# Edge rows of a forward Fourier stage: loaded once, copied on the chip, multiplied last

## The chip, the cores and the metric

The kernel runs on one core of one Trainium2 chip. A core has a matrix engine (TensorE, PE in the profile, with its weight loads listed as PEld), a vector engine (VectorE, DVE), a scalar engine (ScalarE, ACT), a general engine (GpSimd, POOL) and a sync engine (SyncE, SP), each with its own queue of instructions that it takes in order. Sixteen DMA engines move data between HBM and the on-chip memory; a DMA is issued from the queue of one of the engines (here SP, POOL and, for constants, ACT).

The metric is the device time of one execution in microseconds, the median of several executions.

## What is computed

The reference has two layers on a tensor of 4 batches x 512 time steps x 128 x 64. The first layer (normalisations, a decayed scan, two convolutions, a small feed-forward net) isn't touched by the change. The second takes a moving average over time as a trend, mixes the lowest 128 Fourier modes of the remainder with complex weights, and adds both up:

```python
trend = _moving_average(x, KERNEL)      # 25 steps, ends repeated
seasonal = x - trend
xf = jnp.fft.rfft(seasonal, axis=1)
xs = xf[:, :M]                          # M = 128
ys = jnp.einsum('bmnc,cmk->bknc', xs, W)
...
filt = jnp.fft.irfft(yf, n=T, axis=1)
return trend + filt
```

## The kernel before

The second layer is `layer1`. It goes over the four batches in two groups of two (lines 959 to 965). For each group it runs `transform` for both batches, then `mix`, then `invert` for both. All of it is in float32. The products of one group stay in one large on-chip tile `xf`.

`transform` (line 834) is the forward Fourier transform. One batch is cut along its 8192 columns into NS = 16 slabs of SL = 512 columns, so a group has 32 slabs and the whole kernel 64. For a slab:

- `slab` (line 827) loads all 512 time steps of the columns, 1 MB, on SP's queue into a tile `xin`. The pool tag `big` has five buffers.
- A tile `edge` (line 839, pool tag `edge`, two buffers) receives the first 12 and the last 12 time steps of the columns, because the moving average treats the ends of the time axis differently from a circular one and these 24 rows carry the correction. Lines 840 to 842 load the 24 rows twice, to partitions 0 to 23 and to partitions 32 to 55: four DMAs of 24 KB each (12 rows of 2 KB), on POOL's queue. One copy of the rows meets the weights of the real part, the other those of the imaginary part (r = 0 and 1); partitions 32 to 55 are what the profile calls the second row group.
- VectorE folds the time axis: sums and differences `uv` of the halves (line 846, two instructions), then sums and differences `ev` of the quarters of the sum (line 856, two instructions). Each of the tags has two buffers.
- TensorE makes three sets of products into two PSUM tiles `pf[0]` and `pf[1]`. Called E, D and V here: E, the edge products (line 853), four matmuls with 24 rows, which open the sums (`start=True`); D, the odd modes from the differences (line 860), four matmuls onto one half of each `pf`; V, the even modes (line 867), four matmuls onto a quarter each. Every float32 matmul appears twice in the profile, so the profile has eight of each for a slab. The PSUM tag `a` has four buffers, which is two slabs.
- ScalarE copies `pf[0]` and `pf[1]` into `xf` (line 871).

TensorE takes its instructions in the order of the code (`manual_schedule`, line 958): E, D, V of one slab, then E, D, V of the next. The other engines' queues are ordered by the framework's scheduler, which may place an instruction ahead of one from an earlier line. A tile's buffer is written again only when all its readers are done: the loads of `edge` for slab s wait for E of slab s-2, `uv` of slab s for D of slab s-2, and the first product of slab s for the copies of slab s-2 to `xf`.

`mix` (line 873) loads 1 MB of weights at a time into `w`, which shares the tag `big` with `xin` and so waits for old slabs, and negates parts of it on POOL (line 882). `invert` (line 905) goes back to time: per slab it makes the waves, loads `xin` again, loads `halo` rows on SP into the tag `edge` (lines 937 and 940), forms the moving average (lines 943 and 946), adds (line 949) and writes 1 MB out on POOL's queue (line 950).

Of the kernel before, what the change touches and what calls it, by code (L numbers as in the profile page):

```python
# [17 lines left out]
T = 512  # L18
NF = 128
H = 64  # L20
# [10 lines left out]
HALO = KMA // 2  # L31
# [748 lines left out]
def layer1(ctx, tc, x4, wri, dftv, dftd, dfte, idfte, idfto, avg, avgh, out):  # L780
# [7 lines left out]
    nc = tc.nc  # L788
# [9 lines left out]
    def load(name, src):  # L798
        t = const.tile(list(src.shape), F32, name=name)
        nc.scalar.dma_start(t, src)  # L800
        return t

    dftv_sb = load("dftv_sb", dftv)
    dftd_sb = load("dftd_sb", dftd)
    dfte_sb = load("dfte_sb", dfte)
# [5 lines left out]
    def bank(tag):  # L811
        return ps.tile([P, SL], F32, tag=tag, name=tag)


    def by_c(row):
        return row.rearrange("p (a c l) -> p a l c", c=H, l=2)

    def by_n(row):
        return row.rearrange("p (a l c) -> p a l c", c=H, l=2)
# [7 lines left out]
    def slab(b, s):  # L827
        xin = io.tile([P, NT, SL], F32, tag="big", name="xin", bufs=5)
        nc.sync.dma_start(
            xin, x4[b][:, s * SL : (s + 1) * SL].rearrange("(c p) d -> p c d", p=P)  # L830
        )
        return xin

    def transform(b, xf):

        for s in range(NS):
            c = slice(s * SL, (s + 1) * SL)
            xin = slab(b, s)
            edge = io.tile([P, SL], F32, tag="edge", name="edge")
            for r in range(2):  # L840
                nc.gpsimd.dma_start(edge[32 * r : 32 * r + HALO, :], x4[b][0:HALO, c])
                nc.gpsimd.dma_start(edge[32 * r + HALO : 32 * r + 2 * HALO, :], x4[b][T - HALO : T, c])
            uv = []
            for op in (ALU.add, ALU.subtract):
                t = io.tile([P, 2, SL], F32, tag=f"uv{len(uv)}", name="uv")
                nc.vector.tensor_tensor(t, xin[:, 0:2, :], xin[:, 2:4, :], op)  # L846
                uv.append(t)
            pf = [bank("a"), bank("a")]
            for r in range(2):
                at = slice(32 * r, 32 * r + 2 * HALO)  # L850
                for h in range(2):
                    hs = slice(h * H, (h + 1) * H)
                    nc.tensor.matmul(pf[r][hs, :], lhsT=dfte_sb[at, hs], rhs=edge[at, :], start=True, stop=False)  # L853
            ev = io.tile([P, 2, SL], F32, tag="ev", name="ev")
            for k, op in enumerate((ALU.add, ALU.subtract)):
                nc.vector.tensor_tensor(ev[:, k, :], uv[0][:, 0, :], uv[0][:, 1, :], op)
            for i in range(2):
                for r in range(2):
                    h = 1 - r
                    nc.tensor.matmul(  # L860
                        pf[r][h * H : (h + 1) * H, :], lhsT=dftd_sb[:, i, r, :], rhs=uv[1][:, i, :],
                        start=False, stop=(i == 1),
                    )
            for k in range(2):
                for r in range(2):
                    q = r * H + k * H // 2
                    nc.tensor.matmul(  # L867
                        pf[r][q : q + H // 2, :], lhsT=dftv_sb[:, k, r, :], rhs=ev[:, k, :], start=False, stop=True
                    )
            for r in range(2):  # L870
                nc.scalar.copy(by_c(xf[:, r, c]), by_n(pf[r]))

# [85 lines left out]
    with tc.manual_schedule(engines={nc.tensor.engine}):  # L958
        for b0 in range(0, B, G):
            xf = spec.tile([P, G, 2, D], F32, tag="xf", name="xf")  # L960
            for b in range(G):
                transform(b0 + b, xf[:, b, :, :])
            mix(xf)
            for b in range(G):
                invert(b0 + b, xf[:, b, :, :])
# [109 lines left out]
```

## Time and profile before

| | us |
|---|---|
| median of 3 executions | 3868.74 (3863.71 to 3873.1) |
| the profiled execution, own time | 3868.33 |
| its span in the profile | 3866.3 |
| TensorE busy in it | 3643.1 (94%) |
| VectorE busy | 2695.6 (70%) |
| ScalarE busy | 1722.6 (45%) |
| GpSimd busy | 567.9 (15%) |
| all E products, both stages (81.0), D (129.6), V (70.9) | 281.5 |
| first transform stage, first product to the first product of `mix` | 2868.89 to 3004.77 |
| second transform stage, likewise | 3363.38 to 3503.36 |

The page has one row for each engine and a picture of the span in 40 slices. Below that it lists, for groups of equal instructions, the busy time, the mean duration of one, and the idle time just before them with what ended it. A group's busy time counts overlapping instructions once, while the mean is that of one instruction: the 512 edge products have a mean of 626 ns, and yet are busy for 81.0 us, because four of them run side by side on different parts of the array. Of the whole span, the two transform stages, which the change touches, are about 276 us.

### The profile page before, as it was taken

What the parts mean: (1) busy time and instruction counts of PE and PEld (TensorE: products, weight loads), DVE (VectorE), ACT (ScalarE), POOL (GpSimd) and SP (SyncE); (2) the same over time, 40 slices, a digit from 0 to 9 for tenths busy, and PEclk for the clock granted to TensorE, in tenths of its full rate; (3) what the DMA queues carried; (4) which work ended last, traced back from release to release, by engine and by line L of the source; (5) the groups of instructions that cost most, each with busy time, mean ns of one, the idle gap of its engine ahead of it and who ended that gap; (6) DMA issues with size and microseconds to landing.
All of it is one profiled execution on the core that took longest, in us unless ns stands there. A gap on an engine that the chain in (4) does not pass through costs nothing. (4 is left out here: it accounts for less than half of the span.)

```text
span 3866.3 us, 44881 instructions
## 1 busy us (share of the span) xinstructions
PE 3643.1 (94%) x15945; PEld 1343.5 (35%) x15945; DVE 2695.6 (70%) x3498; ACT 1722.6 (45%) x2427; POOL 567.9 (15%) x910
## 2 busy tenths in 40 slices
PE   9999999988999999899999988999989999999999
PEld 4433322233333223333322322333322843326533
DVE  4445669978656896865689799855558267792577
ACT  0023346645556564555656578867742210022100
POOL 0000012211000121110012121100025101141011
PEclk9999999999999999999999999999989999999999
DMA  9767657777765787776568677645559468994587
GB/s 310 262 215 251 222 181 260 258 242 273 255 229 183 235 279 259 248 257 231 191 229 274 215 252 248 213 162 179 182 192 289 145 217 293 314 295 157 191 299 266
DMA packets 432695, 913.86 MB, mean 236 GB/s; under 512 B 36248, under 2 KB 86616, under 8 KB 428376
## 3 DMA queue, kind: packets, MB, share of 16 engines
q1 hardware_dynamic: 350080, 634.55, 49.3%
q0 software_dynamic: 79872, 274.77, 20.3%
q8 instruction: 127, 2.08, 0.2%
q10 hardware_dynamic: 2520, 1.67, 0.1%
q14 instruction: 96, 0.79, 0.1%
HBM read 642.35 MB, written 268.50 MB: 236 GB/s over the span
## 5 line engine op out<-in xcount | busy, mean ns | idle before, releaser
L667 PE MATMUL pa<-mid,w_sb 128*64 128x512 f32 x2048 | 505.9, 615 | 74.0 <-DVE x4t L672 73.5
L660 ACT ACTIVATE mid<-m,fb_sb 128x1024 f32<-128x1024 f32 x256 | 284.5, 1111 | 245.0 <-PE m L656 244.5
L672 DVE SCALAR_TENSOR_TENSOR x4t<-pa,fb_sb,x 128x512 f32<-128x512 f32 x252 | 187.7, 745 | 200.5 <-PE pa L667 200.5
L656 PE MATMUL m<-x,w_sb 64*128 64x512 f32 x1008 | 291.7, 651 | 1.0 <-ACT mid L660 0.7
L660 ACT ACTIVATE mid<-c,fb_sb 128x1024 f32<-128x1024 f32 x256 | 283.0, 1106 | 1.2 <-PE c L656 1.1
L667 PEld LDWEIGHTS pa<-mid,w_sb 128*64 128x64 f32 x2048 | 126.3, 138 | 421.3 <-issue 223.8
L656 PE MATMUL c<-x,w_sb 64*128 64x512 f32 x1008 | 264.1, 597 | 4.7 <-ACT mid L660 4.7
L360 PE MATMUL a<-xp,wx 128*128 128x512 f32 x512 | 246.5, 608 | 6.2 <-DVE wx L357 5.7
L943 PE MATMUL b<-xin,avg_sb 128*128 128x512 f32 x512 | 230.8, 593 | 3.3 <-DVE xin L949 3.3
L949 DVE TENSOR_TENSOR xin<-b,pm 128x512 f32<-128x512 f32 x256 | 159.2, 683 | 96.4 <-PE b L946 81.5
L920 ACT COPY two<-a 128x512 f32<-128x512 f32 x64 | 37.5, 585 | 424.1 <-PE a L915 424.1
L523 ACT ACTIVATE sq<-x 128x1024 f32<-128x1024 f32 x128 | 134.9, 1054 | 200.6 <-DVE x L520 200.6
L564 DVE SCALAR_TENSOR_TENSOR to<-kd,vec,to 128x510 f32<-128x510 f32 (+1 forms) x288 | 210.7, 744 | 18.7 <-ACT to L560 16.9
L633 ACT ACTIVATE kd<-kd,vec 128x512 f32<-128x512 f32 x256 | 193.5, 809 | 7.1 <-DVE kd L625 7.1
L846 DVE TENSOR_TENSOR uv<-xin 128x1024 f32<-128x1024 f32 x128 | 156.3, 1226 | 46.9 <-PE a L860 30.1
L250 PE MATMUL st<-x,ones 128*32 128x512 f32 x512 | 173.7, 606 | 13.8 <-DVE x L520 13.5
L344 DVE BATCH_NORM_STATS2 stt<-wx 128x6 f32<-128x512 f32 x174 | 113.1, 685 | 101.2 <-DMA wx<-in_x 100.7
L825 DVE COPY xf<-b 128x256 f32<-128x256 f32 x128 | 54.4, 425 | 183.2 <-PE b L889 182.6
L681 PEld LDWEIGHTS pt<-ident,x4t 128*128 128x128 f32 x1024 | 108.3, 141 | 210.9 <-ACT mid L660 155.0
L692 POOL DMA_DIRECT2D x<-ob x64 | 49.0, 766 | 899.9 <-ACT ob L688 853.6
L357 DVE TENSOR_SCALAR wx<-wx,vec 128x192 f32<-128x192 f32 x174 | 48.8, 318 | 189.0 <-DMA wx<-in_wkvr 170.9
L482 PE MATMUL a<-rst,wo_sb 64*128 64x512 f32 x512 | 150.5, 662 | 30.8 <-DVE x L484 28.6
(238 smaller groups left out, 6803.4 us busy)
## 6 DMA issues: line engine op xcount, KB each, us to landing
xp<-in_xt SPq DMA_DIRECT2D x256, 512.0 KB
xin<-x SPq DMA_DIRECT2D x128, 1024.0 KB
kh<-to SPq DMA_DIRECT2D x152, 512.0 KB
x<-x POOLq DMA_DIRECT2D x128, 512.0 KB, 4.0
kx<-x SPq DMA_DIRECT2D x128, 512.0 KB
x<-ob POOLq DMA_DIRECT2D x64, 1024.0 KB, 6.6
out<-xin POOLq DMA_DIRECT2D x64, 1024.0 KB, 7.1
x<-x SPq DMA_DIRECT2D x96, 512.0 KB
```

Of the source, the lines that this page charges most:

```text
L250: nc.tensor.matmul(st[32 * q : 32 * q + 32, :], lhsT=ones, rhs=src[:, j, :], start=first, stop=last,)
L360: nc.tensor.matmul(pa[:, k, :], lhsT=wq[:, j, k * P : (k + 1) * P], rhs=xp[:, j, :], start=first and j == 0, stop=last and j == 1,)
L482: nc.tensor.matmul(at[:, j, :], lhsT=wo_sb[js, :], rhs=rst[js, :], start=True, stop=True)
L564: nc.vector.scalar_tensor_tensor(to[:, j, k:], xr[:, j, : SL - k], vec[:, w, c], to[:, j, k:], ALU.mult, ALU.add)
L633: tc.keep_in_program_order(nc.scalar.activation(d[:, j, :], d[:, j, :], AF.Identity, bias=vec[:, B4, c], scale=vec[:, G4, c]))
L656: nc.tensor.matmul(pm[:, h, :], lhsT=w1_sb[hs, m * P : (m + 1) * P], rhs=x3[hs, :], start=True, stop=True)
L660: nc.scalar.activation(mid, pm, AF.Gelu_apprx_tanh, bias=fb1_sb[:, m : m + 1])
L667: nc.tensor.matmul(pa[h * H : (h + 1) * H, :], lhsT=w2_sb[:, m, :], rhs=mid[:, h, :], start=(m == 0), stop=(m == 1),)
L672: nc.vector.scalar_tensor_tensor(x4t, pa, fb2_sb, x3s[c // 2][:, c % 2, :], ALU.add, ALU.add)
L846: nc.vector.tensor_tensor(t, xin[:, 0:2, :], xin[:, 2:4, :], op)
L943: nc.tensor.matmul(po[j], lhsT=avg_sb[:, j, :], rhs=xin[:, j, :], start=True, stop=False)
L949: nc.vector.tensor_tensor(by_n(xin[:, j, :]), by_n(po[j]), by_c(pm[j % 2][:, j // 2, :]), ALU.add)
```

## The change

The 24 edge rows are loaded once, to partitions 0 to 23, with two DMAs in place of four. ScalarE then copies them to partitions 32 to 55. The edge products move from the first place in a slab to the last: D and V now open the sums, and E closes them.

```diff
             edge = io.tile([P, SL], F32, tag="edge", name="edge")
-            for r in range(2):
-                nc.gpsimd.dma_start(edge[32 * r : 32 * r + HALO, :], x4[b][0:HALO, c])
-                nc.gpsimd.dma_start(edge[32 * r + HALO : 32 * r + 2 * HALO, :], x4[b][T - HALO : T, c])
+            nc.gpsimd.dma_start(edge[0:HALO, :], x4[b][0:HALO, c])
+            nc.gpsimd.dma_start(edge[HALO : 2 * HALO, :], x4[b][T - HALO : T, c])
+            nc.scalar.copy(edge[32 : 32 + 2 * HALO, :], edge[0 : 2 * HALO, :])
...
             pf = [bank("a"), bank("a")]
-            for r in range(2):
-                at = slice(32 * r, 32 * r + 2 * HALO)
-                for h in range(2):
-                    hs = slice(h * H, (h + 1) * H)
-                    nc.tensor.matmul(pf[r][hs, :], lhsT=dfte_sb[at, hs], rhs=edge[at, :], start=True, stop=False)
...
                     nc.tensor.matmul(
                         pf[r][h * H : (h + 1) * H, :], lhsT=dftd_sb[:, i, r, :], rhs=uv[1][:, i, :],
-                        start=False, stop=(i == 1),
+                        start=(i == 0), stop=False,
                     )
...
                     nc.tensor.matmul(
-                        pf[r][q : q + H // 2, :], lhsT=dftv_sb[:, k, r, :], rhs=ev[:, k, :], start=False, stop=True
+                        pf[r][q : q + H // 2, :], lhsT=dftv_sb[:, k, r, :], rhs=ev[:, k, :], start=True, stop=False
                     )
+            for r in range(2):
+                at = slice(32 * r, 32 * r + 2 * HALO)
+                for h in range(2):
+                    hs = slice(h * H, (h + 1) * H)
+                    nc.tensor.matmul(pf[r][hs, :], lhsT=dfte_sb[at, hs], rhs=edge[at, :], start=False, stop=True)
```

The built program shows where the scheduler puts things. ScalarE's queue now has the copy for slab s+1 ahead of the two `xf` copies of slab s (copy 0, copy 1, `xf` 0, copy 2, `xf` 1, and so on). POOL's queue has two loads for a slab in place of four; the first negation of `w` stood ahead of the loads of the last three slabs of a group, and now stands ahead of those of the last four. SP's queue is the same, and VectorE's too, but for one `uv` instruction per group that moves by one place. TensorE's queue is the same list with one E (four matmuls) taken from the front of each group's transform and put at its end.

## The prediction

> **What bounds the kernel now.** I read first the groups of instructions for TensorE, then the order of time in a calm part of the first transform stage, then the edge loads one at a time, then the two ends of the second stage.
>
> The groups of instructions, shapes kept apart (form, count, busy us, mean ns, idle before):
>
> ```profile
> L860 PE MATMUL a<-uv,dftd_sb 128*64 128x512 f32 x512 | 129.6, 628 | 0.0
> L853 PE MATMUL a<-edge,dfte_sb 24*64 24x512 f32 x512 | 81.0, 626 | 21.8 <-DMA edge<-x 21.8
> L867 PE MATMUL a<-ev,dftv_sb 128*32 128x512 f32 x512 | 70.9, 627 | 0.0
> L846 DVE TENSOR_TENSOR uv<-xin 128x1024 f32<-128x1024 f32 x128 | 156.3, 1226 | 46.9 <-PE a L860 30.1 <-DMA edge<-x 14.3 <-DMA xin<-x 0.6
> L871 ACT COPY xf<-a 128x512 f32<-128x512 f32 x128 | 73.5, 630 | 234.1 <-PE a L867 234.1
> ```
>
> Only E ever waits for data that TensorE can't hurry (21.8 us; the first 16 are the stage's cold start). One calm slab in order of time (start, busy, instruction, idle before):
>
> ```profile
> 2961.90 1.09 PE L853 MATMUL a<-edge,dfte_sb 24*64 24x512 f32 x8
> 2962.05 1.15 ACT L871 COPY xf<-a 128x512 f32<-128x512 f32 x2 [2.73 <-PE a L867]
> 2962.92 1.94 PE L860 MATMUL a<-uv,dftd_sb 128*64 128x512 f32 x8
> 2963.31 0.50 POOL L841 DMA_DIRECT2D edge<-x  x1 [1.89 <-PE a L853]
> 2964.78 1.07 PE L867 MATMUL a<-ev,dftv_sb 128*32 128x512 f32 x8
> 2964.80 0.51 POOL L842 DMA_DIRECT2D edge<-x  x1
> 2965.78 1.09 PE L853 MATMUL a<-edge,dfte_sb 24*64 24x512 f32 x8
> ```
>
> E takes 1.02 us, D 1.86, V 1.00: a period of 3.88 us without a gap, so TensorE is the bound here. VectorE is close behind (two `uv` of 1.226 and two `ev` of 0.69: 3.83 by the means), and a window over two such slabs has the DMA engines at a share of 0.94. Everything is nearly level, and the edge loads are too: issued 0.32 us after E of slab s ends, the last of the four 1.49 later, they have until E of slab s+2. Where this fails, E is longer or late:
>
> ```profile
> 2892.85 1.40 PE L853 MATMUL a<-edge,dfte_sb 24*64 24x512 f32 x8
> ...
> 2897.04 1.39 PE L853 MATMUL a<-edge,dfte_sb 24*64 24x512 f32 x8
> ...
> 3363.38 1.97 PE L853 MATMUL a<-edge,dfte_sb 24*64 24x512 f32 x4
> ...
> 3367.40 1.97 PE L853 MATMUL a<-edge,dfte_sb 24*64 24x512 f32 x4 [2.05 <-DMA edge<-x]
> 3369.30 3.68 PE L860 MATMUL a<-uv,dftd_sb 128*64 128x512 f32 x8
> ...
> 3374.75 1.09 PE L853 MATMUL a<-edge,dfte_sb 24*64 24x512 f32 x8
> ...
> 3481.64 1.98 POOL L882 TENSOR_SCALAR w<-w 128x256 f32<-128x256 f32 x2 [2.99 <-DMA w<-in_wri]
> ...
> 3488.87 1.49 PE L853 MATMUL a<-edge,dfte_sb 24*64 24x512 f32 x8 [1.91 <-DMA edge<-x]
> ```
>
> Three places: a crowded part early in stage one (period 4.19, the second half of E waits 0.3), the start of stage two (the fourth load stood behind an output DMA on POOL's queue, so D of slab 0 began only at 3369.30, at half clock), and the end of each stage (loads behind the negation of `w`).
>
> **What the Trainium skill says.** "DMA: Bandwidth & Descriptors", section on the SWDGE path: a DMA issued from GpSimd costs about 2.0 us plus its bytes over 436 GB/s, which for 24 KB is 2.06. The trace agrees only when the DMA engines are idle (1.9 to 2.0 us at the end of a stage); under load an edge load takes 4 to 6 us. The same page, on queues, says that an engine changes between queues only at packet boundaries; that fits loads that wait behind the 1 MB of `xin`. "ScalarE: Activation LUTs", under what a table load costs: 186 ns + 0.833 ns per element without pointer operands. For 512 elements this is 613 ns, and the trace has 585 from PSUM (line 920) and 630 (line 871). "TensorE: Matmul & The Clock Gate", Part 1: after idling, the array runs at half clock for about 3.4 us of work. The trace agrees: D takes 3.68 in place of 1.94 after the waits above.
>
> **The change, part by part.**
>
> *Order on TensorE.* The queue is the same list, except that one E (four matmuls) goes from the front of each stage to its back: E, D, V, E, D, V becomes D, V, E, D, V, E. So the period without waits stays 3.88, and V to E and E to D follow each other as before: nothing there. On VectorE one `uv` moves by a place per stage: nothing, it runs about two slabs ahead.
>
> *Two loads less, a copy more: the loop that matters.* Edge loads of slab s+2 still wait for E of slab s. After: 0.32 to the first issue, 0.50 to the second, then landing, then the copy, then E. I asked the landing of each load. In 37 calm slabs, issue to landing, in order of issue, averages 5.37, 5.11, 4.84, 4.57 us: issued half a microsecond apart they land 0.23 apart, behind the same stretch of `xin`. So leaving the last two out brings the landing of the set from 6.1 (1.49 + 4.57) to 5.6 (0.50 + 5.11) after the first issue: 0.45 us sooner, not the 1.0 of issue time. Against this stands the copy, 0.62 (between 0.585 and 0.63), and its two handovers, about 0.1 each (0.07 from V's end to the `xf` copy above). Sum from E's end to E's start: 0.32 + 0.50 + 5.11 + 0.62 + 0.2 = 6.75. What is allowed is 2 x 3.88 - 1.09 = 6.67. Before, E's second half could wait about 0.3 longer: 0.32 + 1.49 + 4.57 = 6.4 against 6.97. So a slack of 0.6 turns into none, and the landing scatters by 0.37.
>
> Two things soften this. With 24 fewer 2 KB rows of 560 a slab, the share of the DMA engines falls from 0.94 to about 0.90, and the landing by perhaps 0.15; and a late E finds `xin` further on (slope of landing about 0.6). I chained the slabs by hand with these numbers: at a mean landing of 4.7 the period is 3.91, at 5.0 it is 3.97, at 5.3 it is 4.06. I take 4.97 and a period of 3.97, 0.09 over. For 41 calm slabs that is +3.7; before, they lost 2.1 (71.0 us for 18 and 90.2 for 23, at 3.88). Net +1.6; bounds -2.1 (no wait left) and +10 (0.3 a slab, from a landing of 5.6).
>
> *ScalarE's queue.* The copy for slab s+1 waits for a DMA with `xf` of slab s behind it. `xf` then ends 1.15 us after the copy, and the first D of slab s+2 needs it at the moment E of s+1 ends, which is 1.09 + 0.1 after the copy. So this wait is level with E's own and adds at most 0.1, which the chaining holds. `mix` waits for the last `xf` as before.
>
> *Crowded part of stage one.* Seven slabs at landing 5.4: before 4.19, after (0.32 + 0.50 + 5.4 + 0.72 + 1.19)/2 = 4.07. -0.8.
>
> *Starts.* In stage one D waits only for `uv` (2868.40) in place of the edge load (2868.89): -0.4. In stage two both loads of slab 0 go ahead of the output DMA (3354.0 and 3354.5, 6.0 to land, copied by 3361.2), so D follows the last line-946 product at 3363.4 in place of 3369.3. Slab 0 then ends near 3369.3 rather than 3374.75; -5.4. But the next loads still meet the full DMA queues (landings of 7.0 and 7.6), which costs about 4.4 of waits where before had 1.9. -3; bounds -5.4 and 0.
>
> *Ends.* The first negation of `w` now stands ahead of four slabs of loads. It waits for `w`, which lands about 6 us after slab 11's `uv` frees the buffer. From the end of D of slab 9: 1.3 + 6.0 + 1.98, two loads 0.5 + 4.6, copy and handovers 0.8: E of slab 12 at 15.2, due at 12.64. A wait of 2.6 and about 1.7 of half clock is 4.3 a stage; before it was 3.2 and 4.0. +1.4; bounds -1 and +4.
>
> Sum: +1.6 - 0.8 - 0.4 - 3 + 1.4 = -1.2. The profiled execution took 3868.33 (span 3866.3 and 2.0 around it), 0.4 below the median; so 3867 to 3867.5. I forecast 3868.
>
> **Rivals.**
> (a) *Slower: the loop through ScalarE closes.* If the landing doesn't fall with the traffic, or the copy and handovers cost 1.0 us rather than 0.8, every slab waits. It decides from a mean landing of about 5.2 on: at 5.4 to 5.6 the period is 4.1 to 4.2, +0.25 x 41 = +10; with -2.1 for the waits it takes over and +2 from the ends it is about +10 in all, 3879. For it: slack of 0.6 gone to none. Against: the second load lands at 5.11 even under today's traffic.
> (b) *Faster: the DMA engines get air.* If the landing falls to 4.5, calm slabs run at 3.88 (-2.1), the starts give 5.4, the crowded part 2 and the ends nothing: -9 or so, 3859. For it: at a share of 0.94 a small relief can shorten a queue a good deal. Against: `xin` is 1 MB of 1.07, and the loads land behind it.
> (c) *No change*, gains of the starts against the lost slack: the forecast.
>
> **How the numbers follow.** No change 0.47, (a) 0.34, (b) 0.19. Runs before spread by 0.13% either way, so some 0.2% (7.7 us) is what can be told from nothing. The range runs from (b) to beyond (a), with the bounds of the calm part and the ends: 3857 to 3886; the forecast's own is 3861 to 3876. By the same cases: faster 0.18, same 0.47, slower 0.35.
>
> **What would show it.** The copy near 0.62 us; second loads landing at 4.9 to 5.1; E to E between 3.92 and 4.0 in calm slabs, with the idle time of E put down to ScalarE's edge copy; D of stage two at once after line 946. A calm period of 3.88 speaks for (b), above 4.05 for (a). It is wrong if the copy waits for something other than its two loads, or if `xf` copies held up by it delay D by more than 0.1.

## The result and the profile after

The changed kernel takes 3860.05 us (median of 20, 3842.84 to 3869.84), the kernel before on the same chip 3868.39 (20, 3861.2 to 3878.31): a ratio of 0.9973, with a 95% interval of 0.9963 to 0.9983. It is 8.3 us faster, where the forecast said no change.

The groups of instructions of the changed kernel, shapes kept apart (form, count, busy us, mean ns, idle before and what ended it). The line numbers have moved: D is now L855, V L862, E L869, and the edge copy L842.

```profile
L846 DVE TENSOR_TENSOR uv<-xin 128x1024 f32<-128x1024 f32 x128 | 155.2, 1228 | 35.2 <-DMA edge<-x 14.7 <-PE a L855 13.5 <-DMA xin<-x 5.1
L855 PE MATMUL a<-uv,dftd_sb 128*64 128x512 f32 x512 | 128.4, 612 | 19.5 <-DMA xin<-x 16.1 <-DVE uv L846 3.4
L869 PE MATMUL a<-edge,dfte_sb 24*64 24x512 f32 x512 | 76.0, 612 | 2.8 <-DMA edge<-x 2.6
L862 PE MATMUL a<-ev,dftv_sb 128*32 128x512 f32 x512 | 68.3, 605 | 0.0
L842 ACT COPY edge<-edge 24x512 f32<-24x512 f32 x64 | 39.5, 618 | 170.0 <-DMA edge<-x 160.6 <-DMA xin<-x 9.4
```

Read E first: 81.0 busy and 21.8 idle have become 76.0 and 2.8. Of the idle time some 16 us is the cold start of the stage, which has only changed its name: the first product is now a D and waits for `xin`. Over the three groups E, D and V the idle time is about the same (21.8 before, 22.3 now). What fell is the time that counts as busy, from 281.5 to 272.7 us: an E whose second half waits, or a product at half clock, counts as a longer one. ScalarE waits 170 us for its edge loads; it has time for that.

A calm slab of the changed kernel in order of time (start, busy, instruction, idle before):

```profile
2909.02 1.09 PE L869 MATMUL a<-edge,dfte_sb 24*64 24x512 f32 x8
...
2910.68 0.50 POOL L840 DMA_DIRECT2D edge<-x  x1 [2.88 <-PE a L869]
...
2911.17 0.51 POOL L841 DMA_DIRECT2D edge<-x  x1
...
2912.90 1.09 PE L869 MATMUL a<-edge,dfte_sb 24*64 24x512 f32 x8
...
2915.61 0.62 ACT L842 COPY edge<-edge 24x512 f32<-24x512 f32 x1 [1.68 <-DMA edge<-x]
...
2916.84 0.66 PE L869 MATMUL a<-edge,dfte_sb 24*64 24x512 f32 x4
```

The loop of the edge buffers can be followed with a finger. The E of 2909.02 ends at 2910.11; the loads go out at 2910.68 and 2911.17; the copy starts at 2915.61 and ends at 2916.23; the E that needs it starts at 2916.84, after the next D and V, so it waits for TensorE and not for the rows. E to E is 3.88 and then 3.94 here.

The start of stage two of the changed kernel, TensorE alone:

```profile
3342.90 1.14 PE L946 MATMUL b<-halo,avgh_sb 12*128 12x512 f32 x8
3343.97 1.94 PE L855 MATMUL a<-uv,dftd_sb 128*64 128x512 f32 x8
```

D follows the last line-946 product at once and at full clock. The last line-946 group before:

```profile
3360.00 3.45 PE L946 MATMUL b<-halo,avgh_sb 12*128 12x512 f32 x8 [1.47 <-DMA halo<-x]
```

From here to the start of D (3369.30) it was 9.3 us, with D at half clock. Of these, 2.3 us are the line-946 group itself (3.45 in place of 1.14), which came after a wait for `halo` and not for edge rows.

The spans of two single profiles mislead here: 3840.8 after and 3866.3 before differ by 25.5 us, of which 13.0 lie in the first layer, which isn't touched. Over all the profiles below that layer took between 2853 and 2876 us, in no order that has to do with the kernel. So I read the two transform stages by themselves: the first from its first `uv` to the first product of `mix`, the second from the start of the last line-946 group to the first product of `mix`. One profile each, beside the medians, in us (the difference is to the kernel before on the same chip):

| kernel | stage one | stage two | sum | median | difference | ratio, 95% |
|---|---|---|---|---|---|---|
| before | 138.7 | 143.4 | 282.1 | | | |
| after | 136.3 | 135.0 | 271.3 | 3860.05 | -8.3 | 0.9973 (0.9963 to 0.9983) |
| after_again | 135.6 | 140.8 | 276.4 | 3860.43 | -9.5 | 0.9975 (0.9965 to 0.9985) |
| copy_alone | 137.3 | 141.9 | 279.2 | 3858.31 | -11.7 | 0.9974 (0.9964 to 0.9983) |
| order_alone | 142.6 | 142.0 | 284.6 | 3866.48 | -3.5 | 0.9992 (0.9978 to 1.0006) |
| after_four | 137.5 | 144.4 | 281.8 | 3869.52 | -0.5 | 1.0 (0.9987 to 1.0013) |
| copy_split | 139.1 | 143.2 | 282.3 | 3870.88 | +1.5 | 1.0001 (0.9989 to 1.0012) |
| copy_act | 139.9 | 143.1 | 283.1 | 3871.6 | +2.2 | 0.9999 (0.9986 to 1.0013) |
| after_twice | 139.2 | 150.5 | 289.7 | 3876.68 | +7.8 | 1.0016 (1.0003 to 1.0029) |
| before_bufs3 | 129.5 | 133.1 | 262.6 | 3846.07 | -23.3 | 0.994 (0.9922 to 0.9958) |
| copy_bufs3 | 130.2 | 136.1 | 266.3 | 3844.76 | -24.7 | 0.9938 (0.9919 to 0.9956) |
| order_bufs3 | 129.4 | 135.2 | 264.6 | 3849.94 | -19.0 | 0.9945 (0.9925 to 0.9964) |
| after_bufs3 | 136.2 | 137.1 | 273.3 | 3859.67 | -9.2 | 0.9972 (0.9959 to 0.9985) |
| before_even1 | 138.5 | 146.9 | 285.4 | 3869.53 | +0.6 | 1.0003 (0.999 to 1.0016) |

The sums follow the medians in the large and scatter by 3 to 5 us in the small (before and before_even1 have the same transform, after and after_again are the same kernel). Between 15 and 20 us of the 23 to 25 that the best kernels gain can be seen in the two stages of one profile.

### The profile page after: what moved, and what is told of

Same layout as the page of the kernel before. It is cut to its first block, busy times and chain, and to the rows that moved or that the text cites. A ratio compares the mean times of both kernels' runs of the same rounds, so it can differ in the third digit from the quotient of the medians.

```text
span 3840.8 us, 44890 instructions
## 1 busy us (share of the span) xinstructions
PE 3619.7 (94%) x15945; PEld 1342.6 (35%) x15945; DVE 2692.2 (70%) x3498; ACT 1764.0 (46%) x2491; POOL 504.2 (13%) x782
## 5 line engine op out<-in xcount | busy, mean ns | idle before, releaser
L523 ACT ACTIVATE sq<-x 128x1024 f32<-128x1024 f32 x128 | 135.0, 1054 | 203.0 <-DVE x L520 203.0
L484 DVE TENSOR_TENSOR x<-a,xp 128x1024 f32<-128x1024 f32 x128 | 156.0, 1219 | 20.9 <-PE a L482 17.6
```

What stands on the lines that cost most here:

```text
L484: nc.vector.tensor_tensor(x1, at, xp, ALU.add)
```

## The experiments

My theory after the result: the loop E of slab s, edge loads, copy, E of slab s+2, closed by the two buffers of `edge`, is about as long as the two slabs of 3.88 us that TensorE gives it. The two loads that are left out make it shorter by more than the copy makes it longer. The rivals: that it is the order of the products which gains (D first at the start of a stage, E free to be late), or that the kernel only moves less data.

**The two halves of the change, and the change with its traffic put back.**

after_again is the changed kernel as it is.

> The changed kernel once more, for a second profile. In the first pair of profiles 13.0 us of the difference lay ahead of the first transform stage, in code that is the same in both, and 10.8 in the two transform stages (138.7 + 143.4 us before, measured from the first uv to the first product of mix and from the last line-946 group to the first product of mix; 136.3 + 135.0 after). Theory A (the gain is in the transform stages): the two stages again sum to 269 to 274 us and the time is 8 to 12 us below before, while the part ahead of them differs at random. Theory N (the gain is drift of the untouched layer): the stages sum to 280 or more.

order_alone has E last, but the four loads of before and no copy:

```diff
-            nc.gpsimd.dma_start(edge[0:HALO, :], x4[b][0:HALO, c])
-            nc.gpsimd.dma_start(edge[HALO : 2 * HALO, :], x4[b][T - HALO : T, c])
-            nc.scalar.copy(edge[32 : 32 + 2 * HALO, :], edge[0 : 2 * HALO, :])
+            for r in range(2):
+                nc.gpsimd.dma_start(edge[32 * r : 32 * r + HALO, :], x4[b][0:HALO, c])
+                nc.gpsimd.dma_start(edge[32 * r + HALO : 32 * r + 2 * HALO, :], x4[b][T - HALO : T, c])
```

> Four loads and no copy as before; only the edge products move to the end of a slab. Theory A1 (the place of the edge products brings the gain: D can start a stage without them, and at the end of a stage they come 2.9 us later): -6 to -10 us, stages sum to 272 to 276. Theory A2 (the two missing loads bring it, by less traffic and less queueing on GpSimd): within 3 us of before, sum near 282.

copy_alone is the other half: the two loads and the copy in the kernel before, whose E stays first (the same lines the other way round).

> Two loads and the ScalarE copy, but the edge products first in a slab as before. A1: no gain, or a loss of up to 8 us, since the copy is added to a load that a slab's first products wait for. A2: -6 to -10 us, stages sum to 272 to 276.

after_four is the changed kernel with two further loads of the same rows to partitions that nobody reads:

```diff
             nc.gpsimd.dma_start(edge[HALO : 2 * HALO, :], x4[b][T - HALO : T, c])
+            nc.gpsimd.dma_start(edge[64 : 64 + HALO, :], x4[b][0:HALO, c])
+            nc.gpsimd.dma_start(edge[64 + HALO : 64 + 2 * HALO, :], x4[b][T - HALO : T, c])
             nc.scalar.copy(edge[32 : 32 + 2 * HALO, :], edge[0 : 2 * HALO, :])
```

The copy does not wait for the two further loads: in the trace it starts 0.14 us after the second landing, which is 0.06 ahead of the third and 0.28 ahead of the fourth (medians).

> The changed kernel with two more loads of the same 24 rows for each slab, to partitions 64 to 87 that nothing reads, issued ahead of the copy: the traffic and GpSimd's issue time of before with the order and the copy of after. A1: keeps most of the gain, -5 to -9 us. A2: loses it, within 3 us of before. In calm slabs the landing of the second load then says what the traffic is worth: 4.3 to 4.6 us as in the changed kernel if nothing, 5.1 as before if all of it.

Measured: copy_alone carries the whole gain (0.9974), order_alone none that its interval can tell from nothing, and the change with its loads put back is level with before. So the order as the cause falls, and the loads remain. This rests on the times; the stages of the single profiles are less clear. after_again has a sum of 276.4, between the 274 of theory A and the 280 of theory N, and copy_alone has 279.2 where A2 expected 272 to 276. Since no product and no copy waits for the two further loads of after_four, what they cost is their bytes or the time that GpSimd's queue takes to issue them; after_four doesn't tell these apart.

**Bytes or issues.** copy_split is copy_alone with each load cut into two over half the columns: the bytes of the change, the four issues of before.

```diff
-            nc.gpsimd.dma_start(edge[0:HALO, :], x4[b][0:HALO, c])
-            nc.gpsimd.dma_start(edge[HALO : 2 * HALO, :], x4[b][T - HALO : T, c])
+            for q in range(2):
+                cq = slice(s * SL + q * SL // 2, s * SL + (q + 1) * SL // 2)
+                eq = slice(q * SL // 2, (q + 1) * SL // 2)
+                nc.gpsimd.dma_start(edge[0:HALO, eq], x4[b][0:HALO, cq])
+                nc.gpsimd.dma_start(edge[HALO : 2 * HALO, eq], x4[b][T - HALO : T, cq])
```

> As copy_alone (24 rows loaded once, copied by ScalarE, edge products first), but each of the two loads cut into two of half the columns: four issues on GpSimd and four completions as before, 1 KB rows, the bytes of after. Theory B1 (what the change saves is bytes and the DMA engines' time for them): keeps the gain, ratio 0.996 to 0.999. Theory B2 (it saves issues: the last load of a set goes out 1.49 us after the first rather than 0.50, so the set lands later): ratio 0.999 to 1.001, and in calm slabs the set lands about 6.0 us after the first issue as before, against 4.8 to 5.1 in after and copy_alone.

The gain is gone (1.0001), as B2 expected. The bytes alone do not make it. The DMA part of the profile, for 60 us of calm slabs in stage one, shows what the loads do; the columns of these rows are the count, KB each and the median us from issue to landing. The kernel before:

```profile
q1 hardware_dynamic: 7918, 15.73, 84.1%
q0 software_dynamic: 1897, 1.48, 8.1%
...
edge<-x POOLq DMA_DIRECT2D x60, 24.0 KB, 5.0
```

after_again:

```profile
q1 hardware_dynamic: 8085, 16.04, 89.6%
q0 software_dynamic: 1014, 0.78, 4.0%
...
edge<-x POOLq DMA_DIRECT2D x32, 24.0 KB, 4.4
```

copy_split:

```profile
q0 software_dynamic: 1923, 0.75, 4.7%
...
edge<-x POOLq DMA_DIRECT2D x61, 12.0 KB, 4.2
```

The edge loads' queue (q0) falls from 8.1% of the engines' time to 4.0%, and the large loads (q1) take what comes free. The engines are about as busy as before, and yet the edge loads land sooner. The next table has means over the slabs from 45 to 105 us into each of the two stages, all in us. The landing is given for each load in order of issue. The set is from the first issue to the last landing. "With copy" adds the copy's 0.62 and two handovers of 0.1 where there is a copy. "From E" adds the time from the end of E to the first issue, 0.32 to 0.35 in the kernels without a copy and 0.53 to 0.57 in those with one, and so is the whole loop. In after_four the copy waits for the first two loads alone, so its loop is reckoned with these (5.30). The last column is what the 18 slabs from the tenth to the 28th took beyond 3.88 each, both stages together.

| kernel | landing of each load | set | with copy | from E | calm slabs lose |
|---|---|---|---|---|---|
| before | 5.35, 5.09, 4.81, 4.54 | 6.03 | 6.03 | 6.35 | 2.0 |
| order_alone | 5.32, 5.06, 4.78, 4.49 | 5.98 | 5.98 | 6.33 | 2.1 |
| after | 4.79, 4.57 | 5.06 | 5.88 | 6.45 | 4.5 |
| after_again | 4.63, 4.34 | 4.83 | 5.65 | 6.22 | 1.5 |
| copy_alone | 4.58, 4.31 | 4.80 | 5.62 | 6.17 | 0.5 |
| copy_split | 4.55, 4.26, 3.99, 3.70 | 5.20 | 6.02 | 6.57 | 2.5 |
| after_four | 5.05, 4.80, 4.53, 4.25 | 5.74 | 6.12 | 6.69 | 7.0 |
| after_twice | 4.32, 4.00 | 4.49 | 5.93 | 6.46 | 11.5 |

copy_split has the four loads and about the calm pace of before, with half the bytes, and each of its loads lands 0.8 us sooner. So a single load's landing went here by the bytes of edge rows and not by the number of loads. But its last load is issued a microsecond later than that of copy_alone, its set ends 0.40 later, and its loop is no shorter than that of before (6.57 and 6.35); the time is that of before too. B2's own mark, a set of 6.0, did not come: the set is 5.20, and the copy makes up the rest. after_four has the bytes back, and its second load lands at 4.80 where that of after_again lands at 4.34. Its calm slabs lose 5.0 more than those of before; it is level in time because its starts gain as much (the tenth D of a stage comes 1.7 and 3.4 us sooner, when the 1.02 us of an E that no longer stands ahead of it are taken off).

**A longer loop.** after_twice makes the copy twice, and nothing else:

```diff
             nc.scalar.copy(edge[32 : 32 + 2 * HALO, :], edge[0 : 2 * HALO, :])
+            nc.scalar.copy(edge[32 : 32 + 2 * HALO, :], edge[0 : 2 * HALO, :])
```

> The changed kernel with the ScalarE copy made twice in a row, the second the same as the first: 0.62 us more on the way from the landing to the second half of the edge products, no more traffic and no more issues. If the loop from E over load and copy to E two slabs later sets the calm and filling slabs, the set then takes about 4.95 + 1.24 + 0.2 = 6.4 us from the first issue, more than the 6.03 of before: the gain is lost or turned, 0 to +8 us against before. If copies on ScalarE are hidden, it stays at -10 us.

0.62 us more in the loop makes the change slower than the kernel before (1.0016, interval 1.0003 to 1.0029). Its E group:

```profile
L870 PE MATMUL a<-edge,dfte_sb 24*64 24x512 f32 x512 | 90.8, 616 | 5.8 <-ACT edge L843 3.2 <-DMA edge<-x 2.4
```

90.8 busy against 76.0 with one copy: the second half of E waits inside the group. The loss is in the calm slabs, 11.5 us against 2.0 before. The loop is only 6.46 by the table, since the landing is lower where slabs run late (4.00 against 4.34 in after_again); so the sum shows where the time goes and isn't by itself a forecast of it. The `xf` copies also stand behind the copies on ScalarE; what they add in this run isn't separated.

**The loop opened.** before_bufs3 is the kernel before with a third buffer for `edge` and its tag mate `halo`; the tile `two` of `invert` gives up a buffer to make room.

```diff
-            edge = io.tile([P, SL], F32, tag="edge", name="edge")
+            edge = io.tile([P, SL], F32, tag="edge", name="edge", bufs=3)
...
-            two = io.tile([P, SL], F32, tag="even", name="two")
+            two = io.tile([P, SL], F32, tag="even", name="two", bufs=1)
...
-            halo = io.tile([P, SL], F32, tag="edge", name="halo")
+            halo = io.tile([P, SL], F32, tag="edge", name="halo", bufs=3)
```

> The kernel before with a third buffer for the edge tile (and one in place of two for a small tile of the inverse transform, to make room): the loads go out one slab, 3.9 us, earlier, so their landing no longer decides. Theory C1 (the loop from E over the load to E two slabs later is what costs, and the change gains by shortening it): gains as much as the change or more, -8 to -14 us, with no E over 1.15 us in slabs 2 to 26 of a stage. Theory C2 (the gain is elsewhere, in traffic or in chance): within 3 us of before.

before_even1 is the control: only the line with `two`.

> A control for the kernels with three edge buffers: before with only the small tile of the inverse transform cut from two buffers to one, the edge tile still with two. If the gain of before_bufs3 is the third edge buffer's, this is within 4 us of before; if the smaller tile brought it, -20 us.

The control does nothing (1.0003); the third buffer gives -23.3 us, with the four loads of before, about twice what C1 expected. The buffer serves `halo` in `invert` as well, but what follows the two transform stages took 718.2 us before and 716.4 in before_bufs3 (716.5 in the changed kernel), so at most 2 of the 23 us come from there. Of the 19.5 that its profile shows in the stages, 10.3 lie ahead of the tenth D, 2.0 in the calm slabs and 7.2 at the ends. Two slabs of before_bufs3 from the crowded part of stage one, in order of time:

```profile
2904.85 1.09 PE L853 MATMUL a<-edge,dfte_sb 24*64 24x512 f32 x8
...
2908.73 0.21 PEld L853 LDWEIGHTS a<-edge,dfte_sb 24*64 24x64 f32 x8 [0.84 <-issue]
2908.73 1.09 PE L853 MATMUL a<-edge,dfte_sb 24*64 24x512 f32 x8
...
2912.61 0.21 PEld L853 LDWEIGHTS a<-edge,dfte_sb 24*64 24x64 f32 x8 [0.84 <-issue]
```

The weight loads of E wait for nothing that the profile shows ("issue"), and E comes every 3.88. From the second slab on, the whole of stage one keeps that period to within 0.01, its end too; stage two does so from the third slab on, after one E to E of 10.93. The loads land later than before (mean 5.76 to 5.45, a set of 7.0, the DMA engines at 1.02 in place of 0.93), and it costs nothing, since they have a slab more time. Its E group:

```profile
L853 PE MATMUL a<-edge,dfte_sb 24*64 24x512 f32 x512 | 72.8, 623 | 18.0 <-DMA edge<-x 18.0
```

72.8 is E with hardly a wait in it: two of its 64 slabs have an E of more than 1.15 us, where 18 had one before. So of the 81.0 of before some 8 were waits inside E and half clock; its 18.0 of idle time are little more than the cold start.

copy_bufs3 is copy_alone with the same three lines.

> copy_alone with the third buffer. C1: no better than before_bufs3, since the shorter load set then gains nothing, both -8 to -14 us. C2: keeps its own -10 us and adds nothing.

order_bufs3 is order_alone with them.

> Three edge buffers, four loads, no copy, edge products last. With the loop open the place of the products can only act at the first slabs of a stage: -20 to -28 us against before, within 5 us of before_bufs3.

Once the loop is open, two loads fewer gain nothing more that can be told: copy_bufs3 3844.76, before_bufs3 3846.07 and order_bufs3 3849.94 have overlapping intervals. That speaks against less traffic as a gain of its own, though with six, five and six runs a gain of a few us could hide. copy_bufs3 has the lowest median, and with before_bufs3 it beats both kernels of this study.

**Two misses.** after_bufs3 is the changed kernel with the third buffer.

> The changed kernel with three edge buffers. With the loop open two loads less and the copy are worth nothing in calm slabs, so -20 to -28 us against before, within 5 us of order_bufs3. If less traffic counts of itself, it is 5 us or more below order_bufs3.

It gained nothing over the changed kernel (-9.2 us against before, where the changed kernel had -8.3 and -9.5). Either half of the change alone keeps the buffer's gain (copy_bufs3 -24.7, order_bufs3 -19.0); the copy and E last together lose most of it. The trace of after_bufs3, in order of time, suggests why:

```profile
2901.22 1.09 PE L869 MATMUL a<-edge,dfte_sb 24*64 24x512 f32 x8
...
2905.04 0.62 ACT L842 COPY edge<-edge 24x512 f32<-24x512 f32 x1 [2.27 <-DMA edge<-x]
...
2905.68 1.15 ACT L871 COPY xf<-a 128x512 f32<-128x512 f32 x2
...
2906.69 1.24 PEld L855 LDWEIGHTS a<-uv,dftd_sb 128*64 128x64 f32 x8 [0.81 <-ACT xf L871]
2906.69 2.12 PE L855 MATMUL a<-uv,dftd_sb 128*64 128x512 f32 x8
...
2994.41 0.62 ACT L842 COPY edge<-edge 24x512 f32<-24x512 f32 x1 [5.97 <-DMA edge<-x]
2995.05 1.12 ACT L871 COPY xf<-a 128x512 f32<-128x512 f32 x2
2995.72 3.78 PE L855 MATMUL a<-uv,dftd_sb 128*64 128x512 f32 x8 [2.39 <-ACT xf L871]
```

The E of 2901.22 ends at 2902.31, and its `xf` copies could run then. On ScalarE's queue the edge copy of a later slab stands ahead of them; it waits 2.27 us for its loads, `xf` runs at 2905.68, and D, which needs the PSUM buffer that `xf` empties, takes 2.12 in place of 1.94, its weight loads stretched to 1.24. Other slabs lose up to 0.6 us in the same way. The great loss is at the ends of the stages, where the edge loads stand behind the negation of `w`: at 2994.41 the copy has waited 5.97 us, and D starts 2.39 us late and at half clock. E to E is 8.18 us there and 9.76 at the same place of stage two, 10.2 over the period together, about the 10.7 by which the stages of after_bufs3 exceed those of before_bufs3. With E first (copy_bufs3) the copies to `xf` come after V, and the same place takes 4.12 and at most 4.67. This is read from the trace; no run took that queue order alone away.

copy_act issues the two loads of copy_alone from ScalarE's queue:

```diff
-            nc.gpsimd.dma_start(edge[0:HALO, :], x4[b][0:HALO, c])
-            nc.gpsimd.dma_start(edge[HALO : 2 * HALO, :], x4[b][T - HALO : T, c])
+            nc.scalar.dma_start(edge[0:HALO, :], x4[b][0:HALO, c])
+            nc.scalar.dma_start(edge[HALO : 2 * HALO, :], x4[b][T - HALO : T, c])
```

> copy_alone with the two loads issued from ScalarE's queue in place of GpSimd's. Nothing of the edge rows then stands behind the negations of w and the output DMAs. If those are worth what the ends of the stages show (3 to 4 us each at the end of both stages) it is 6 to 8 us below copy_alone, about -16 us against before. If the copy that waits for a landing holds up the loads behind it on the same queue, it is slower than copy_alone.

The ends of the stages run clean (E to E 3.88 throughout), as the loads no longer stand behind the negation of `w`, but it wins nothing (0.9999). ScalarE's rows of copy_act in the crowded part, ACTq being its queue for DMAs:

```profile
2886.94 0.62 ACT L842 COPY edge<-edge 24x512 f32<-24x512 f32 x1 [2.79 <-DMA edge<-x]
...
2887.04 0.30 ACTq L840 DMA_DIRECT2D edge<-x  x1
...
2892.34 0.62 ACT L842 COPY edge<-edge 24x512 f32<-24x512 f32 x1 [3.34 <-DMA edge<-x]
...
2892.44 0.30 ACTq L840 DMA_DIRECT2D edge<-x  x1
```

Each load goes out only with the copy ahead of it, and that waits for its own loads: the loads of two slabs no longer overlap, and crowded slabs of stage one take 5.3 to 6.9 us each.

## Why the prediction was right or wrong

The measured 3860.05 lies in the range of 3857 to 3886 and far from the forecast of 3868; it is the time of rival (b), 3859, which had 0.19. That rival took a landing of 4.5, and the landing came to 4.57 and 4.34. That the sum came so near is in part luck: (b) had the calm slabs gain 2.1 us and the ends nothing, while in the two profiles of the changed kernel the calm slabs lose 2.5 and gain 0.5, and the ends gain 4.1 and lose 2.8. Step by step:

- **The loop that matters: the place was right, a size wrong.** The prediction found the loop through the two edge buffers and named a late second half of E as its sign. What failed is the relief of the landing: "the landing by perhaps 0.15", hence "I take 4.97 and a period of 3.97". The second load landed at 4.57 and 4.34, a relief of 0.5 to 0.75. With 0.57 from E's end to the first issue (assumed 0.32), the set of 4.95 (mean of the two profiles of the changed kernel), and 0.82 for copy and handovers, the loop takes 6.3, not 6.75, of the 6.67 that are allowed. The later first issue, 0.25 us, was not foreseen and takes back part of the relief. The argument behind the small value was that the edge loads land behind the 1 MB of `xin`; the runs show that their own bytes, under 5% of those moved in a calm window less, count for much more than that share.
- **The tolerance for a late copy was thought gone, and stayed.** Only the second half of E, which reads the copied rows, waits for the copy; the first starts on the loaded rows. The trace has such E at 1.31 in place of 1.09, with the weight loads of E put down to ScalarE in part (3.3 us) and E itself to the loads. One sign of being wrong did come: after a late E, `xf` copies that stand behind the edge copy delay D by more than 0.1. D takes 2.07 to 2.12 in place of 1.94 in 16 slabs of the first profile.
- **The calm part:** predicted +1.6 to its account, measured +2.5 in the first profile of the changed kernel and -0.5 in the second (from the tenth to the 28th slab of both stages). So the main gain isn't there but ahead of it. The set from 15 to 45 us into a stage falls from 6.75 to 5.68 and 5.51. By the tenth D, less the 1.02 of an E that no longer stands ahead of it, stage one has gained 3.1 and 3.0, where 1.2 was predicted for start and crowded slabs, and stage two 6.1 and 5.0, where the bound was 5.4 and 3 was taken. In stage two all of this is the start (7.2); the slabs behind it take 1.1 and 2.2 longer than before, as the prediction had said of them.
- **The start of stage two** went as described: D right behind line 946. From the start of the line-946 group to D it is 1.07 us, in order_alone as well. Much of it comes with the two loads too: in copy_alone, with E first, it is 2.7 us, against 9.3 before; but in before_even1 it is 10.8 and in copy_split 5.1, so this step scatters.
- **The ends** scatter more than the step of +1.4 that was put on them: between 0.3 and 6.5 us a stage over before, before_even1 and the changed kernel's two profiles. The moved negation can't be priced from one profile.
- **Costs that held:** the copy (0.618 for 0.62), which also agrees with 613 ns, the estimate for 512 elements from what the Trainium skill, "ScalarE: Activation LUTs", under what a table load costs, gives for an ACTIVATE without pointer operands; a period of 3.88 whatever the order of E, D and V; nothing that can be told from the order of the products alone (0.9992, interval 0.9978 to 1.0006). Its one profile shows two things that cancel: by the same count the tenth D's come 3.6 us sooner in all, and the ends take 5.8 longer, with one E to E of 10.73.
- **Rival (a)** did not happen, but its mechanism is real: after_twice closes the loop with one more copy, at about the price that (a) set (+7.8 for +10), and in the calm slabs, as (a) had it.
- **A slip without weight:** the bytes of a slab were 1.09 MB before and are 1.05 now by the rows that the prediction counts, and not 1.07.

What stays open: why half the edge bytes shorten a load's landing by a half microsecond while the engines are as busy as before; why the crowded slabs of stage one gain, when their loop from E's end to E's start is 7.1 us before and, with copy and later issue, still 7.1 and 6.9 in the two profiles after; and how the 8 to 12 us divide exactly between starts, crowded slabs and ends, which one profile each can't settle.

## What to carry to other kernels

When every slab of a level pipeline waits a little for a small load, write down the loop from the reader that frees the buffer to the reader that needs it, in time, and hold it against the period times the buffers: one third buffer of a small tile was worth 23 us here, the saved loads 8 to 12, and both together no more that could be told than the buffer. Price a small load under traffic from its landing in the trace, with a wide bound on how it changes when its own queue empties. A copy that waits for a DMA is best kept off a queue where something urgent stands behind it: by their traces that is what after_bufs3 and copy_act paid for.

## What the runs showed of the hardware

- Leaving out half of the small loads lowered the landing of each of the others by 0.5 to 0.75 us (5.09 to 4.57 and 4.34), while the share of the DMA engines was 0.91 and 0.94, against 0.93 before. The Trainium skill, "DMA: Bandwidth & Descriptors", section on the SWDGE path, gives 2.06 us as an estimate for such a load (2.0 plus its bytes over 436 GB/s); the second loads here took 4.3 to 5.1, so under this traffic it does not hold.
- Cutting a load in two on GpSimd's queue didn't change how soon the first pieces landed (4.55 and 4.26 against 4.58 and 4.31), but each issue holds the queue for 0.50 us, and with two issues more the gain was gone. From ScalarE's queue the issues took 0.30 and 0.38 us by the median, and one 0.95.
- The untouched first layer, up to the first `uv`, took from 2853 to 2876 us in the profiles of kernels that don't differ there: a spread larger than the effect that was looked for.
